# Two layers of attention: normalisation of the output split over two blocks, image loads in halves, another order of the units

## The chip, the cores and the metric

The kernel runs on one core of one Trainium2 chip. The metric is the device time of one execution in microseconds; the runs of one kernel are summed up by their median. All arithmetic is in fp32.

## The reference, cut to what matters

Each of two layers adds to x the result of an attention over the group-normalised x. There are 16 images of 256 channels and 32 x 32 positions, four heads of 64 channels.

```python
def layer(x, Wq, bq, Wk, bk, Wv, bv, rel_h, rel_w):
    xf = gn(x).reshape(b, c, n)                  # 16 groups over the last axis
    q, k, v = (W @ xf + bias, split into 4 heads of 64)
    sim  = einsum('bhdi,bhdj->bhij', q, k)
    rel  = (rel_h + rel_w).reshape(heads, d, n)
    qpos = einsum('hdi,bhdj->bhij', rel, q)
    attn = softmax(sim + qpos, axis=-1)
    out  = einsum('bhdn,bhmn->bhdm', v, attn)
    return x + out.reshape(x.shape)
x = layer(x, *layer0); x = layer(x, *layer1)
```

## The kernel before, in words

**Units and blocks.** A unit is one image in one layer, (b, l). There are 32 of them, in the order of the list `units` (line 139). A unit has four blocks: two pairs of heads (`pr`) times two halves of 512 query positions (`half`). `block(n)` (line 610) writes the instructions of block n, 128 blocks in all. Even blocks have half 0, odd blocks half 1. In an even block the text speaks of the "first" (b = 0) or "third" (b = 2) block of a unit, in an odd one of the second or fourth.

**One block.** For each of eight tiles j of 128 keys: VectorE writes the positional part of the scores into a PSUM tile (`seed`, line 344), TensorE adds k times q to it (`scores`, line 380), and ScalarE takes the exp into an SBUF tile p (line 389). `attend` (line 414) multiplies p by v into `po` in two stretches, and `take_out` (line 475) copies it into an output tile `od`. The PSUM tiles have four tags, a to d, given out by the list `ring`; a seed has to wait until the tile's former use has been read out. Beside that, each block works ahead for the next units: projections, values and positions (lines 263, 293, 321), and on ScalarE and TensorE the group norm of the units after (`norm_sums`, `norm_squares`, `norm_apply`, small matmuls `pm` at line 208). Each block holds two such pieces of projections on TensorE.

**The sums of the softmax.** VectorE adds up the p tiles of j = 0 to 6 in `acc` (`add_up`, lines 398 and 400); the add of j = 6 of an even block is issued at the start of the next block, that of an odd block at its end. POOL adds the last one by an accumulating DMA (`add_last`, line 431), then `acc` is folded over the partitions by further DMAs: `fold` (line 436), `stack_up` on SP's queue (line 450), `fold_again` (line 455), `fold_stack` (line 460, five times), `spread_sums` on SP's queue (line 468) into `den_all`. These stretch over the following three blocks.

**Normalisation.** In an even block n, for the pair of blocks n-4 and n-3 (`before`, line 616): after the scores of j = 5, `reciprocals` (line 504) takes the reciprocal on VectorE (line 511), writes it to DRAM (`rd`, line 513) and reads it back broadcast in two DMAs of 256 KB (`rden`, line 518), all three on SP's queue. Near the end of the same block `finish` (line 523) multiplies `od` by it (line 530), adds bias and residual into x (line 532) and, in layer 1, writes the result to DRAM (line 534). On VectorE's queue three seeds of the next block follow.

**Loads.** An image x is loaded by two DMAs of 512 KB (`load_x`, line 103) into one of five buffers. The load is issued in the fourth block of the unit three places ahead of the image's first unit (line 719).

**Order.** The order of the program's text is the order of each engine's queue: VectorE, ScalarE, TensorE, POOL with its DMAs, and SP with its DMAs. Each works through its queue in order, and waits at semaphores. The two stretches of a matmul group are separated by a token that POOL writes (`stretches`, line 155; `word`, line 164), so a late POOL queue can hold TensorE up. The last unit's second half has a path of its own (`block_without_pieces`, line 748), where `keep_sums` (line 492) carries sums.

Of the kernel before, what the change touches and what calls it, by code (L numbers as in the profile page):

```python
# [9 lines left out]
F32 = mybir.dt.float32  # L10
# [3 lines left out]
ALU = mybir.AluOpType  # L14
# [3 lines left out]
P = 128  # L18
HALF = 512
# [24 lines left out]
def flat(ap):  # L44
    return ap.rearrange("p w h -> p (w h)")
# [7 lines left out]
def fast_path(ctx, tc, sh, x, layers, out, W, den_all, token, good, flag):  # L53
# [26 lines left out]
    nc = tc.nc  # L80
    B, C, H, N, CC, NT, NH, D, GT = (
        sh.B, sh.C, sh.H, sh.N, sh.CC, sh.NT, sh.NH, sh.D, sh.GT
    )
# [4 lines left out]
    xpool = ctx.enter_context(tc.tile_pool(name="xpool", bufs=5))  # L88
# [4 lines left out]
    ppool = ctx.enter_context(tc.tile_pool(name="ppool", bufs=12))  # L93
# [3 lines left out]
    opool = ctx.enter_context(tc.tile_pool(name="opool", bufs=2))  # L97
# [2 lines left out]

    xt = {}

    def load_x(b):
        xt[b] = xpool.tile([P, CC, N], F32, tag="x", name=f"x_{b}")
        for cc in range(CC):
            nc.sync.dma_start(xt[b][:, cc, :], flat(x[b, cc * P : (cc + 1) * P]))

    def load_raw(name, parts):
# [27 lines left out]
            nc.scalar.copy(w.rearrange("p a c -> p (a c)"), raw_t.pop((l, part)))  # L136


    units = [(b, 0) for b in range(4)] + [(0, 1), (1, 1)]
    for b in range(4, B - 1):  # L140
        units += [(b, 0), (b - 2, 1)]
    units.insert(-1, (B - 1, 0))
    units += [(b, 1) for b in range(B - 3, B)]
    NU = len(units)
    ks, qs, abt, vts, xns = {}, {}, {}, {}, {}

# [190 lines left out]
    seeds, probs, accs, outs = {}, {}, {}, {}  # L337
# [54 lines left out]
    def add_up(blk, j):  # L392
        u, pr, half = blk
        if j == 0:
            return
        if j == 1:
            accs[blk] = apool.tile([P, 2, HALF], F32, tag="acc", name=f"acc_{u}_{pr}_{half}")
            nc.vector.tensor_tensor(accs[blk], probs[blk, 0], probs[blk, 1], ALU.add)  # L398
        else:
            nc.vector.tensor_tensor(accs[blk], accs[blk], probs[blk, j], ALU.add)  # L400

    QUART = HALF // 2
# [22 lines left out]
    index, rdens = {}, {}  # L425
# [44 lines left out]
    def take_out(blk, po):  # L470

        u, pr, half = blk
        if half == 0:
            outs[u, pr] = opool.tile([P, 3, HALF], F32, tag="od", name=f"od_{u}_{pr}")
        nc.scalar.copy(  # L475
            outs[u, pr][:, half, :].rearrange("p (a n) -> p a n", a=2), po[:, :, :QUART]
        )
# [11 lines left out]
                        start=True, stop=True, tile_position=(0, r0), skip_group_check=True,  # L489
                    )  # L490

    def keep_sums(od, po, n, count):
        rows_ = slice(0, 2 * count * R)
        nc.scalar.copy(
            od[rows_, 2, :].rearrange("p (a n) -> p a n", a=2), po[rows_, :, QUART:]
        )
        for x in range(count):
            for h in range(2):
                r0 = (2 * x + h) * R
                nc.sync.dma_start(  # L500
                    den_all[h * D : (h + 1) * D, n + x, :], od[r0 : r0 + 1, 2, :]
                )

    def reciprocals(u, pr, count=2):
# [15 lines left out]
                rd[h : h + 1].to_broadcast([D, count * HALF]),  # L520
            )

    def finish(u, pr):

        b, l = units[u]
        xs = xt[b][:, pr, :]
        od = outs.pop((u, pr))
        o = od[:, 0:2, :].rearrange("p x (k e) -> p x k e", e=8)
        rden = rdens.pop((u, pr)).rearrange("p (k x e) -> p x k e", x=2, e=8)
        nc.vector.tensor_tensor(o, o, rden, ALU.mult)  # L530
        o = od[:, 0:2, :].rearrange("p a n -> p (a n)")
        nc.vector.scalar_tensor_tensor(xs, o, W.bv[l][:, pr : pr + 1], xs, ALU.add, ALU.add)  # L532
        if l == NL - 1:
            nc.sync.dma_start(flat(out[b, pr * P : (pr + 1) * P]), xs)


    def finish_half(u, pr, half, o, rden):
# [35 lines left out]
    blocks = [(u, pr, half) for u in range(NU) for pr in range(CC) for half in range(NH)]  # L573
# [4 lines left out]
    pos = {}  # L578
# [31 lines left out]
    def block(n):  # L610
        blk = blocks[n]
        u, b = divmod(n, BPU)
        half = blk[2]

        stacked = blocks[n - 3][:2] if half == 1 and n > 2 else None
        before = blocks[n - 4][:2] if half == 0 and n > 3 else None
        after = blocks[n + 1] if n + 1 < len(blocks) else None
        previous = blocks[n - 1] if n > 0 else None
        one, two = u + 1 < NU, u + 2 < NU

        pieces = u + 1 < NU or b < 2
        if u + 1 == NU and b == 1:
            widen(u, 1)
        f0, f1, f2, f3 = ring
        folded = n - 1 < FOLDED
        if not pieces:
            return block_without_pieces(n, half)

        if stacked:
            fold_stack(*stacked, D)  # L630
        if previous:
            if half == 1:
                add_up(previous, 6)
            if folded:
                add_last(previous)
            else:
                add_up(previous, 7)
        for j in range(1, 4):
            scores(blk, j)
        (first, first_out), (second, second_out) = prepare(u, b)  # L640
        first(0)
        if b == 0 and one:
            norm_apply(u + 1, range(0, 1))
        if b == 1 and two:
            norm_sums(u + 2, range(9, 11))
        seed(blk, 4, f1)
        scores(blk, 4)
        add_up(blk, 1)
        if b == 0 and one:
            norm_apply(u + 1, range(1, 5))  # L650
        if b == 1 and two:
            norm_sums(u + 2, range(11, 12))
        if b == 2 and two:
            norm_squares(u + 2, range(0, 5))
        second(0)
        if half == 1:
            second_out()
        first.word()
        if half == 0:
            second.word()  # L660
        if stacked:
            fold_stack(*stacked, R)
        if previous and folded:
            fold(previous)
        if stacked:
            fold_stack(*stacked, R // 2)
            fold_stack(*stacked, R // 4)
        first(1)
        first_out()
        seed(blk, 5, f0)  # L670
        scores(blk, 5)
        if before:
            reciprocals(*before)
        if previous and folded:
            stack_up(previous)
        add_up(blk, 2)
        if half == 0:
            second(1)
            second_out()
        seed(blk, 6, f1)  # L680
        scores(blk, 6)
        if half == 0:
            ring[2:] = f3, f2
        seed(blk, 7, ring[2])
        scores(blk, 7)
        add_up(blk, 3)
        add_up(blk, 4)

        if after:
            seed(after, 0, f0)  # L690
        if n in check:
            next(checks)
        if b == 0 and one:
            norm_apply(u + 1, range(5, 9))
        if b == 0 and two:
            norm_sums(u + 2, range(0, 2))
        if b == 1 and two:
            norm_sums(u + 2, range(12, G))
        if b == 1 and one:
            norm_apply(u + 1, range(9, 11))  # L700
        if b == 2 and two:
            norm_squares(u + 2, range(5, 11))
        po = psum2(ring[3], f"po_{n}")
        values_of_p = attend(blk, po)
        values_of_p(0)
        if two and half == 1:
            mean, mean_out = (norm_mean if b == 1 else norm_var)(u + 2, zeroed(f1, f"pm_{n}"))
            mean(0)
        if after:
            scores(after, 0)  # L710
        values_of_p.word()
        if two and half == 1:
            mean(1)
        if stacked:
            fold_stack(*stacked, R // 8)
            spread_sums(*stacked)
        if previous and folded:
            fold_again(previous)
        if b == 3 and u + 3 < NU and units[u + 3][0] not in xt:
            load_x(units[u + 3][0])  # L720
        if two and half == 1:
            mean_out()
        add_up(blk, 5)
        if half == 1:
            add_up(blk, 6)
        if before:
            finish(*before)
        if after:
            for j in range(1, 4):
                seed(after, j, ring[j % 3])  # L730
        if b == 0 and two:
            norm_sums(u + 2, range(2, 9))
        if b == 1 and one:
            norm_apply(u + 1, range(11, G))
        if b == 2 and two:
            norm_squares(u + 2, range(11, G))
        values_of_p(1)
        take_out(blk, po)
        pos[n] = po

# [7 lines left out]
    def block_without_pieces(n, half):  # L748

        blk = blocks[n]  # L750
        u, pr, _ = blk
        f0, f1, f2, f3 = ring
        summed = blocks[n - 2][:2] if half == 0 else (u, pr)
        before = blocks[n - 4][:2] if half == 0 else blocks[n - 3][:2]
        first = index[summed + (0,)]
        add_up(blocks[n - 1], 7)
        for j in range(1, 4):
            scores(blk, j)
        sums_of_p(blocks[first:n], pos[n - 1])
        keep_sums(outs[summed], pos[n - 1], first, n - first)  # L760
        if half == 1:
            finish(*before)
        else:
# [451 lines left out]
```

## Time and profile before

| what | value |
|---|---|
| median of 3 runs | 2587.51 us (2584.55 to 2592.39) |
| profiled execution, its own time | 2584.54 us |
| its span, first to last instruction | 2582.8 us |
| granted TensorE clock, mean | 0.995 |
| busy: TensorE, weight loads | 2533.4 us (98%), 1699.2 us |
| busy: VectorE, ScalarE, POOL | 2264.9, 1959.6, 827.4 us |
| mean of the DMAs | 86 GB/s |

The profile is that of one execution. "PE" is TensorE's matmuls, "PEld" its weight loads, DVE VectorE, ACT ScalarE, POOL GpSimd, SP SyncE; "SPq" is a DMA issue on SP's queue. Groups are named by line, engine and tiles (out<-in). A matmul's end is modelled, so busy TensorE says that it was never without work, not that it ran at its peak.

### The profile page before, as it was taken

The numbers are of one execution on the slowest core, as the hardware profiler recorded it, in microseconds if no ns is written. First come the engines' busy times: TensorE is split into PE (matmuls) and PEld (weight loads), VectorE is DVE, ScalarE is ACT, GpSimd is POOL, SyncE is SP. The second block draws the span as 40 slices with busy tenths as digits, with TensorE's granted clock in tenths as the row PEclk, the third lists the DMA queues.
The fourth block names the chain that finished last, engine by engine and source line by source line (L and its number), as shares of the span: only waits on it lengthen the run. The fifth ranks groups of instructions, "written<-read, shape, count | busy, mean of one in ns | idle before, by whom it ended". The sixth has DMA issues, their size and how long they took to land. (4 is left out here: it accounts for less than half of the span.)

```text
span 2582.8 us, 86091 instructions
## 1 busy us (share of the span) xinstructions
PE 2533.4 (98%) x37474; PEld 1699.2 (66%) x37474; DVE 2264.9 (88%) x2076; ACT 1959.6 (76%) x3934; POOL 827.4 (32%) x1254
## 2 busy tenths in 40 slices
PE   8999999999999999999999999999999999999998
PEld 4666766667667655675657767676666677666654
DVE  6788888888888998978889898888898898998997
ACT  6778777787777887776877778777788777787653
POOL 1233333323333333333333332333323333323320
PEclk9999999999999999999999999999999999999999
DMA  3444444444444444444444444444444444444441
GB/s 90 81 69 79 80 86 82 91 100 78 93 86 94 90 76 99 88 87 86 80 93 87 96 83 84 99 86 91 81 81 105 93 87 82 72 83 83 87 89 49
DMA packets 119538, 221.06 MB, mean 86 GB/s; under 512 B 53736, under 2 KB 55272, under 8 KB 119152
## 3 DMA queue, kind: packets, MB, share of 16 engines
q0 software_dynamic: 53568, 129.58, 30.6%
q1 hardware_dynamic: 65584, 85.90, 12.3%
q8 instruction: 295, 4.83, 0.8%
q14 instruction: 91, 0.75, 0.1%
HBM read 51.78 MB, written 17.30 MB: 27 GB/s over the span
## 5 line engine op out<-in xcount | busy, mean ns | idle before, releaser
L344 DVE TENSOR_TENSOR ps<-abt 128x1024 f32<-128x1024 f32 x1018 | 1222.3, 1229 | 232.2 <-ACT p L389 66.3
L389 ACT ACTIVATE p<-ps,shift 128x1024 f32<-128x1024 f32 x1024 | 1094.2, 1114 | 348.4 <-PE ps L380 257.4
L380 PE MATMUL ps<-q,k 64*64 64x512 f32 x8192 | 1027.1, 594 | 17.9 <-DVE ps L344 17.2
L414 PE MATMUL po<-p,v 64*64 64x256 f32 x16384 | 945.8, 376 | 0.1
L414 PEld LDWEIGHTS po<-p,v 64*64 64x64 f32 x16384 | 807.1, 133 | 155.3 <-issue 44.6
L400 DVE TENSOR_TENSOR acc<-acc,p 128x1024 f32<-128x1024 f32 x644 | 781.9, 1214 | 7.3
L380 PEld LDWEIGHTS ps<-q,k 64*64 64x64 f32 x8192 | 396.1, 133 | 344.8 <-issue 173.6
L460 POOL DMA_DIRECT2D stack<-stack x310 | 254.0, 819 | 498.9 <-DMA stack<-stack 262.7
L164 POOL MEMSET token<- 1x1 f32 x380 | 43.4, 114 | 861.5 <-PE po L414 488.0
L293 PE MATMUL pv<-Wv,xn 64*64 64x256 f32 x4096 | 251.4, 376 | 0.3 <-DVE var L868 0.3
L263 PE MATMUL pq<-xn,Wq 64*64 64x512 f32 x2048 | 251.3, 592 | 0.3 <-DVE xn L900 0.3
L263 PE MATMUL pk<-xn,Wk 64*64 64x512 f32 x2048 | 248.9, 590 | 0.0
L455 POOL DMA_DIRECT2D stack<-acc x248 | 225.1, 1111 | 71.9 <-DMA stack<-acc 50.5
L293 PEld LDWEIGHTS pv<-Wv,xn 64*64 64x64 f32 x4096 | 201.2, 133 | 56.1 <-issue 41.5
L243 ACT ACTIVATE xn<-x,nshift,rstd 128x128 f32<-128x128 f32 x496 | 210.9, 500 | 9.7 <-POOL nshift L234 9.7
L188 ACT ACTIVATE junk<-x,neg 128x128 f32<-128x128 f32 x498 | 195.1, 401 | 0.0
L263 PEld LDWEIGHTS pq<-xn,Wq 64*64 64x64 f32 x2048 | 107.7, 134 | 113.0 <-issue 108.5
L436 POOL DMA_DIRECT2D acc<-acc x124 | 102.3, 825 | 241.1 <-DMA acc<-p 219.2
L475 ACT COPY od<-po 128x512 f32<-128x512 f32 x127 | 74.4, 586 | 128.4 <-PE po L414 119.9
L263 PEld LDWEIGHTS pk<-xn,Wk 64*64 64x64 f32 x2048 | 98.4, 134 | 102.9 <-issue 101.8
L431 POOL DMA_DIRECT2D acc<-p x124 | 143.4, 1156 | 50.4 <-ACT p L389 40.1
L398 DVE TENSOR_TENSOR acc<-p,p 128x1024 f32<-128x1024 f32 x128 | 156.2, 1221 | 0.1
(75 smaller groups left out, 1231.3 us busy)
## 6 DMA issues: line engine op xcount, KB each, us to landing
acc<-p POOLq DMA_DIRECT2D x124, 512.0 KB, 5.3
rden<-rd SPq DMA_DIRECT2D x126, 256.0 KB, 4.7
acc<-acc POOLq DMA_DIRECT2D x124, 256.0 KB, 3.9
x<-in_x_dram SPq DMA_DIRECT2D x32, 512.0 KB, 4.6
stack<-acc SPq DMA_DIRECT2D x248, 64.0 KB, 2.1
stack<-acc POOLq DMA_DIRECT2D x248, 64.0 KB, 2.9
out_dram<-x SPq DMA_DIRECT2D x31, 512.0 KB, 3.5
stack<-stack POOLq DMA_DIRECT2D x62, 128.0 KB, 2.7
```

The source lines that it names most:

```text
L188: nc.scalar.activation(junk, grouped(xt[units[u][0]], g), func, accum_out=into[:, g : g + 1], **bias)
L243: nc.scalar.activation(grouped(xns[u], g), grouped(xt[units[u][0]], g), AF.Identity, bias=shift[:, g : g + 1], scale=rstd[:, g : g + 1],)
L263: yield nc.tensor.matmul(pk[c, nh, :], w[l][rs, cc, c0 : c0 + D], xns[u][rs, cc, nh * HALF : (nh + 1) * HALF], start=(t == 0 and cc == 0), ...
L293: yield nc.tensor.matmul(pv[c, a, i, :], xns[u][rs, cc, j0 : j0 + D], W.wv[l][rs, cc, :], start=(t == 0 and cc == 0 and i == 0), stop=(t = ...
L344: nc.vector.tensor_tensor(ps.rearrange("p h (w y) -> p h w y", y=H), ab[:, :, :H].unsqueeze(2).to_broadcast([P, 2, XH, H]), ab[:, :, H + h ...
L380: nc.tensor.matmul(ps[c, h, :], a[hs, j0 : j0 + D], b[hs, columns], start=bool(tag) and i == 0, stop=i == len(terms) - 1, skip_group_check ...
L389: nc.scalar.activation(p, ps, AF.Exp, bias=W.shift)
L398: nc.vector.tensor_tensor(accs[blk], probs[blk, 0], probs[blk, 1], ALU.add)
L400: nc.vector.tensor_tensor(accs[blk], accs[blk], probs[blk, j], ALU.add)
L414: yield nc.tensor.matmul(po[c, a, :QUART], vts[u][rs, j, c0 : c0 + D], p[rs, h, a * QUART : (a + 1) * QUART], start=(t == 0 and j == 0), s ...
L455: nc.gpsimd.dma_start(at, acc[R:D, h, :], accum_op=ALU.add)
L460: nc.gpsimd.dma_start(stack[:rows_], stack[rows_ : 2 * rows_], accum_op=ALU.add)
```

## The change

The order of the units is rewritten: some layer-1 units come earlier, others later. Images are loaded one half per odd block instead of both in the fourth block. `finish` is split: `normalise` near the start of the odd block n, `add_residual` near its end, for the pair of blocks n-5 and n-4. `reciprocals` moves within the even block from after the scores of j = 5 to after the adds of j = 3 and 4. The add of j = 6 is issued at the start of the next block for odd blocks also. `od` tiles have two parts of 512 instead of three and three buffers instead of two; the sums kept at the end lie in a p tile.

```diff
@@ -100,9 +100,10 @@
 
     xt = {}
 
-    def load_x(b):
-        xt[b] = xpool.tile([P, CC, N], F32, tag="x", name=f"x_{b}")
-        for cc in range(CC):
+    def load_x(b, parts=range(CC)):
+        if 0 in parts:
+            xt[b] = xpool.tile([P, CC, N], F32, tag="x", name=f"x_{b}")
+        for cc in parts:
             nc.sync.dma_start(xt[b][:, cc, :], flat(x[b, cc * P : (cc + 1) * P]))
 
     def load_raw(name, parts):
@@ -136,11 +137,12 @@
             nc.scalar.copy(w.rearrange("p a c -> p (a c)"), raw_t.pop((l, part)))
 
 
-    units = [(b, 0) for b in range(4)] + [(0, 1), (1, 1)]
-    for b in range(4, B - 1):
+
+    units = [(b, 0) for b in range(4)] + [(0, 1), (1, 1), (4, 0), (2, 1), (3, 1), (5, 0)]
+    for b in range(6, B - 4):
         units += [(b, 0), (b - 2, 1)]
-    units.insert(-1, (B - 1, 0))
-    units += [(b, 1) for b in range(B - 3, B)]
+    units += [(B - 6, 1), (B - 4, 0), (B - 3, 0), (B - 5, 1), (B - 2, 0), (B - 1, 0)]
+    units += [(b, 1) for b in range(B - 4, B)]
     NU = len(units)
     ks, qs, abt, vts, xns = {}, {}, {}, {}, {}
 
@@ -471,7 +473,7 @@
 
         u, pr, half = blk
         if half == 0:
-            outs[u, pr] = opool.tile([P, 3, HALF], F32, tag="od", name=f"od_{u}_{pr}")
+            outs[u, pr] = opool.tile([P, 2, HALF], F32, tag="od", name=f"od_{u}_{pr}", bufs=3)
         nc.scalar.copy(
             outs[u, pr][:, half, :].rearrange("p (a n) -> p a n", a=2), po[:, :, :QUART]
         )
@@ -489,16 +491,15 @@
                         start=True, stop=True, tile_position=(0, r0), skip_group_check=True,
                     )
 
-    def keep_sums(od, po, n, count):
+    def keep_sums(po, n, count):
         rows_ = slice(0, 2 * count * R)
-        nc.scalar.copy(
-            od[rows_, 2, :].rearrange("p (a n) -> p a n", a=2), po[rows_, :, QUART:]
-        )
+        d = ppool.tile([P, 2, HALF], F32, tag="p", name=f"d_{n}")[:, 0, :]
+        nc.scalar.copy(d[rows_].rearrange("p (a n) -> p a n", a=2), po[rows_, :, QUART:])
         for x in range(count):
             for h in range(2):
                 r0 = (2 * x + h) * R
                 nc.sync.dma_start(
-                    den_all[h * D : (h + 1) * D, n + x, :], od[r0 : r0 + 1, 2, :]
+                    den_all[h * D : (h + 1) * D, n + x, :], d[r0 : r0 + 1, :]
                 )
 
     def reciprocals(u, pr, count=2):
@@ -520,18 +521,23 @@
                 rd[h : h + 1].to_broadcast([D, count * HALF]),
             )
 
-    def finish(u, pr):
+    def normalise(u, pr):
+        o = outs[u, pr].rearrange("p x (k e) -> p x k e", e=8)
+        rden = rdens.pop((u, pr)).rearrange("p (k x e) -> p x k e", x=2, e=8)
+        nc.vector.tensor_tensor(o, o, rden, ALU.mult)
+
+    def add_residual(u, pr):
 
         b, l = units[u]
         xs = xt[b][:, pr, :]
-        od = outs.pop((u, pr))
-        o = od[:, 0:2, :].rearrange("p x (k e) -> p x k e", e=8)
-        rden = rdens.pop((u, pr)).rearrange("p (k x e) -> p x k e", x=2, e=8)
-        nc.vector.tensor_tensor(o, o, rden, ALU.mult)
-        o = od[:, 0:2, :].rearrange("p a n -> p (a n)")
+        o = outs.pop((u, pr)).rearrange("p a n -> p (a n)")
         nc.vector.scalar_tensor_tensor(xs, o, W.bv[l][:, pr : pr + 1], xs, ALU.add, ALU.add)
         if l == NL - 1:
             nc.sync.dma_start(flat(out[b, pr * P : (pr + 1) * P]), xs)
+
+    def finish(u, pr):
+        normalise(u, pr)
+        add_residual(u, pr)
 
 
     def finish_half(u, pr, half, o, rden):
@@ -610,10 +616,11 @@
     def block(n):
         blk = blocks[n]
         u, b = divmod(n, BPU)
-        half = blk[2]
+        pr_, half = blk[1:]
 
         stacked = blocks[n - 3][:2] if half == 1 and n > 2 else None
-        before = blocks[n - 4][:2] if half == 0 and n > 3 else None
+        summed = blocks[n - 4][:2] if half == 0 and n > 3 else None
+        before = blocks[n - 5][:2] if half == 1 and n > 4 else None
         after = blocks[n + 1] if n + 1 < len(blocks) else None
         previous = blocks[n - 1] if n > 0 else None
         one, two = u + 1 < NU, u + 2 < NU
@@ -629,14 +636,15 @@
         if stacked:
             fold_stack(*stacked, D)
         if previous:
-            if half == 1:
-                add_up(previous, 6)
+            add_up(previous, 6)
             if folded:
                 add_last(previous)
             else:
                 add_up(previous, 7)
         for j in range(1, 4):
             scores(blk, j)
+        if before:
+            normalise(*before)
         (first, first_out), (second, second_out) = prepare(u, b)
         first(0)
         if b == 0 and one:
@@ -669,8 +677,6 @@
         first_out()
         seed(blk, 5, f0)
         scores(blk, 5)
-        if before:
-            reciprocals(*before)
         if previous and folded:
             stack_up(previous)
         add_up(blk, 2)
@@ -685,6 +691,8 @@
         scores(blk, 7)
         add_up(blk, 3)
         add_up(blk, 4)
+        if summed:
+            reciprocals(*summed)
 
         if after:
             seed(after, 0, f0)
@@ -716,15 +724,13 @@
             spread_sums(*stacked)
         if previous and folded:
             fold_again(previous)
-        if b == 3 and u + 3 < NU and units[u + 3][0] not in xt:
-            load_x(units[u + 3][0])
+        if half == 1 and u + 3 < NU and units[u + 3][1] == 0 and u > 0 or n == 3:
+            load_x(units[u + 3][0], range(pr_, pr_ + 1) if u > 0 else range(CC))
         if two and half == 1:
             mean_out()
         add_up(blk, 5)
-        if half == 1:
-            add_up(blk, 6)
         if before:
-            finish(*before)
+            add_residual(*before)
         if after:
             for j in range(1, 4):
                 seed(after, j, ring[j % 3])
@@ -753,11 +759,13 @@
         summed = blocks[n - 2][:2] if half == 0 else (u, pr)
         before = blocks[n - 4][:2] if half == 0 else blocks[n - 3][:2]
         first = index[summed + (0,)]
+        if half == 0:
+            add_up(blocks[n - 1], 6)
         add_up(blocks[n - 1], 7)
         for j in range(1, 4):
             scores(blk, j)
         sums_of_p(blocks[first:n], pos[n - 1])
-        keep_sums(outs[summed], pos[n - 1], first, n - first)
+        keep_sums(pos[n - 1], first, n - first)
         if half == 1:
             finish(*before)
         else:
```

## The prediction

> **What bounds the kernel now.** I read the page first, then the waits, the timelines of the engines and the windows of single stretches.
>
> ```profile
> PE 2533.4 (98%) x37474; PEld 1699.2 (66%) x37474; DVE 2264.9 (88%) x2076; ACT 1959.6 (76%) x3934; POOL 827.4 (32%) x1254
> ...
> rden<-rd SPq DMA_DIRECT2D x126, 256.0 KB, 4.7
> acc<-acc POOLq DMA_DIRECT2D x124, 256.0 KB, 3.9
> x<-in_x_dram SPq DMA_DIRECT2D x32, 512.0 KB, 4.6
> ```
>
> TensorE is busy nearly throughout, so the change can win only what TensorE loses in stalls. To size that I took from ScalarE's timeline the start of the second exp (tile p of j=1) of each of the 128 blocks; below T is that moment of the even block of a pair (half 0), and T+20.66 that of its odd block. Undisturbed, the four blocks of a unit take 20.66, 18.26, 20.64 and 18.28 us, together 77.84 us. The windows of such blocks show no gap at all:
>
> ```profile
> 2177.26:2197.93 20.67, 20.67 (x292) 13.96 (x288) 17.86 (x17) 17.39 (x39) 7.65 (x10) 1.00 0.44 82
> 2197.93:2216.20 18.27, 18.27 (x300) 11.89 (x296) 17.25 (x17) 15.83 (x34) 8.13 (x13) 1.00 0.45 77
> ```
>
> The first column after the window is its length, the second TensorE's busy time: they are equal, so no reordering makes such a block shorter. What the first 31 units take beyond that is 44.2 us: 19.4 in first, 20.5 in second, 4.3 in fourth blocks of a unit, nothing in third ones. The last unit adds 91.8 us with gaps of its own. The waits name two causes:
>
> ```profile
> PEld ps L380 <- DVE ps L344: 150.7, 335, 4.2
> PEld pm L208 <- POOL token L164: 42.2, 60, 3.7
> DVE od L530 <- DMA rden<-rd: 32.2, 18, 5.0
> DVE r L511 <- DMA den_all<-stack: 19.2, 22, 2.1
> ```
>
> (waiter, releaser: total us, times, longest.) **Stall A**: VectorE waits at `finish` for the broadcast reciprocals `rden`; the seeds of the next block are queued behind it, and TensorE waits for the seeds. The worst case is the first block of unit 14:
>
> ```profile
> 1155.60 1.22 DVE L400 TENSOR_TENSOR acc<-acc,p 128x1024 f32<-128x1024 f32 x1
> 1161.86 1.23 DVE L530 TENSOR_TENSOR od<-od,rden 128x1024 f32<-128x1024 f32 x1 [5.04 <-DMA rden<-rd]
> 1163.12 1.28 DVE L532 SCALAR_TENSOR_TENSOR x<-od,bv,x 128x1024 f32<-128x1024 f32 x1
> 1164.33 3.50 DVE L344 TENSOR_TENSOR ps<-abt 128x1024 f32<-128x1024 f32 x3
> ```
>
> ```profile
> 1163.00:1165.50 2.50, 0.00 (x0) 0.00 (x0) 2.46 (x4) 0.59 (x1) 1.69 (x2) 0.76 0.30 57
> 1165.50:1171.00 5.50, 5.39 (x28) 1.71 (x32) 5.50 (x6) 2.23 (x2) 1.74 (x2) 0.50 0.49 130
> ```
>
> TensorE stands still and then works at half its clock (0.50). All large A stalls are in the first block of a unit, which follows a load of two 512 KB halves of x. Here rden was asked for early and came late because its predecessor `rd` (8 KB) landed only with the 512 KB accumulate `acc<-p` of the same block:
>
> ```profile
> 1155.49 0.84 POOL L436 DMA_DIRECT2D acc<-acc  x1 [7.17 <-DMA acc<-p]
> ```
>
> SP's timeline has the two rden issues at 1155.38, just when that accumulate ended. **Stall B**: in an odd block, the second stretch of the small matmul `pm` waits for a token that POOL writes only after a string of stack folds; a fold chain that starts late delays it. From first and fourth blocks' excess and the gap that opens each, I assign A 27 us (19.4 plus about 8 that spill into the following block) and B 17 us.
>
> [...] a wait of 4.2 us was followed by 0.50, a wait of 2.1 us was not. [...]
>
> **The change, part by part.**
>
> 1. *Residual in two parts, one block later; add of j=6 of odd blocks one block later.* VectorE's work per pair is the same; it moves. Occupancies from the timeline: seed or add 1.14, normalise 1.26, residual 1.20, reciprocal 0.17. Even block before: 8 seeds, 5 adds, reciprocal, finish: 17.4 us of 20.66; odd: 8 seeds, 7 adds: 17.1 of 18.26. After: even 8+6, reciprocal: 16.1; odd 8+6, finish: 18.4 of 18.26. The odd block overruns by 0.1 us, so it must start early, and it can. The clean pair reads
>
> ```profile
> 2190.71 1.22 DVE L400 TENSOR_TENSOR acc<-acc,p 128x1024 f32<-128x1024 f32 x1
> 2192.26 1.23 DVE L530 TENSOR_TENSOR od<-od,rden 128x1024 f32<-128x1024 f32 x1 [0.33 <-DMA rden<-rd]
> 2193.52 1.29 DVE L532 SCALAR_TENSOR_TENSOR x<-od,bv,x 128x1024 f32<-128x1024 f32 x1
> 2194.72 3.50 DVE L344 TENSOR_TENSOR ps<-abt 128x1024 f32<-128x1024 f32 x3
> 2198.12 1.22 DVE L400 TENSOR_TENSOR acc<-acc,p 128x1024 f32<-128x1024 f32 x1
> 2199.26 1.23 DVE L344 TENSOR_TENSOR ps<-abt 128x1024 f32<-128x1024 f32 x1
> ```
>
> Without finish, the first two of the three seeds follow at 2191.9; the third waits for the exp of score 0 (ends 2194.73), so it runs 2194.8 to 2195.9, the add of j=6 to 2197.1, normalise to 2198.3. Seed 4 cannot start before the exp of score 1 ends (2199.04); it starts now at 2199.26. So normalise fits, with about 0.9 us over: it may start as late as T+20.75 without moving a seed. Later costs TensorE one for one, since seed 7 is ready now only some 0.1 us before its score. The residual takes the place of the moved add (1.20 for 1.14) ahead of a 0.96 us idle. In the even block the moved add sits before seed 4, which then ends about 0.44 us before its score. Cost: 0. Bounds: 0 to 0.3 us in each of 62 pairs, if these margins fail.
>
> 2. *Reciprocal later.* It now comes after the add of j=4, at T+12.3 instead of T+4.6; the three DMAs follow on SP behind stack_up, which waits for POOL's fold. Today the fold is issued at T+6.5 (third block) or T+7 to 8.5 (first block) and takes 3.4 us alone, 4.4 to 5.3 with rden in flight; stack_up issues at T+10 to 14. With rden gone from there I take 3.4 us. First block: fold T+8.6, stack_up T+12.1 and 12.6, rd T+13.2, landing 1.6 later at T+14.8, two rden landing 4.9 after the first issue: T+19.7. Third block: the moved add delays acc<-p from T-2 to T+1.6, it lands at about T+6.6 to 7.8, so the fold is hardly later; rden lands at T+18.5 to 19. Both are ahead of T+20.75, by 1.0 and 2 us. Not shown by the trace is rden in that slot: 4.4 us at best (in three blocks, where the fold was missing or came late, both had landed 4.4 to 4.6 after the first issue), 6.4 at worst as beside a fold: T+19.2 to T+21.2. The reciprocal's own wait of 19.2 us ends; it was covered mostly. A goes: -27. I keep +4: x of image 3 is still loaded whole before block 4, where the chain gives about 1.3 us late, and some loads start late.
>
> 3. *Loads in halves.* 512 KB instead of 1 MB start before an even block. With 1 MB ahead, acc<-p took 6.3 to 9.7 us instead of 4.7 in eleven of twelve cases; I estimate 5.0 to 6.5 with half. The out DMAs move too: behind the later residual and SP's spread and load, they leave at the start of the next even block instead of at T+17. In the alternating part, units that load and units that write alternate, so there is one 512 KB transfer per even block. Both are inside the fold time taken above.
>
> 4. *B.* The accumulate of the even block no longer waits until T+22.3 for the add of j=6; that add ends 2.2 us earlier, so its fold clears earlier in the chain, and the out DMA that slowed fold_again (landing at T+22 instead of T+19.7) is gone. Against it, rden now runs beside fold_again: about 1 us, absorbed by POOL's own wait for TensorE at T+24. I take -17 and keep +5.
>
> 5. *Order of units, three od buffers, sums kept in a p tile.* ScalarE's 8.5 us of waits for od end, unseen by TensorE. Every load finds a buffer freed at least a block before. The tail: normalise joins `widen`, but finish left the block before; one more add ahead of the sums of the next: within 0.5 us, taken as 0.
>
> Sum against the profiled execution, 2584.5 (span 2582.8 and 1.7 around it): 2584.5 - 27 + 4 - 17 + 5 = 2549.5. It lies 3.0 us under the median of the runs shown (2587.5), so a median may be 0 to 3 us higher: I say 2551.
>
> **Rivals.** *Slower: rden comes too late for normalise.* The chain is now serial: fold, stack_up, rd, rden in 7.5 us after the reciprocal, where it had 10 us before. If the new slot is as crowded as the old one in first blocks (fold 5.3, rd 3.5, rden 5.9), rden lands at T+24; halfway to that, at T+22.75, 31 first blocks lose 2.0 us each: 2549.5 + 62 = 2612. The gain is gone from a mean lateness of 0.57 us over 62 pairs (35/62). For it: SP's strict order. Against it: the fold and the accumulate, which held rd and rden up, have landed by then. *Half gain:* lateness of some 0.5 us in first blocks (+15) and B only halved (+4): 2569. *No effect:* new collisions of loads and writes at the start of even blocks make stalls as large as the old ones: about 2585.
>
> **How the numbers follow.** Forecast 0.64 (2540 to 2561), half gain 0.18 (to 2579), no effect 0.04, slower 0.14. A measurement of this kernel can tell about 0.3%, 7.8 us, from no change: faster 0.82, same 0.05, slower 0.13. The range 2538 to 2579 holds the first two.
>
> **What would show it.** Right: no wait of `od` on rden over 1 us after block 4, rden landing before T+20.75, reciprocal's wait gone, clock never 0.50 between 200 and 2400 us, PE waits for POOL's token in `pm` below half of 42 us. Wrong: waits of normalise on rden in most odd blocks, or acc<-p landing beyond T+10 in many first blocks.

## The result, and the profile after

| | before | changed |
|---|---|---|
| median of 5 runs | 2585.83 us (2583.91 to 2592.39) | 2566.39 us (2564.16 to 2574.49) |
| profiled execution, its time | 2584.54 us | 2564.16 us |
| its span | 2582.8 us | 2562.4 us |
| mean granted clock | 0.995 | 0.998 |

The ratio is 0.9928, with a 95% interval of 0.9907 to 0.995: faster by 0.7%. The forecast was 2551, in a range of 2538 to 2579: it lies inside, but the gain is 19 us where 35 were forecast.

Measured by the same block starts as before the change, the first 31 units exceed 31 x 77.84 us, here called the floor, by 23.8 us instead of 44.2. First blocks, which had 19.4 us of excess, have 0.7; fourth blocks have 8.2 instead of 4.3, second ones 14.9 instead of 20.5. So the stalls at the end of even blocks are gone, but the odd blocks together still lose 23.1 us where they lost 24.8. The waits of the changed kernel (waiter, releaser: total us, times, longest) say by what:

```profile
PEld ps L382 <- DVE ps L346: 145.1, 303, 2.9
DVE od L527 <- DMA rden<-rd: 54.5, 37, 3.7
PEld pm L210 <- POOL token L166: 27.3, 60, 2.9
```

The wait of VectorE for the broadcast reciprocals, 32.2 us in 18 places before, is now 54.5 us in 37 places; the wait of the reciprocal for the sums (19.2 us) is gone. The token waits of the small matmuls fell from 42.2 to 27.3 us; these are waits of the weight loads, which start ahead of their matmuls (by 0.28 us at the median of these 60 waits in the changed kernel). TensorE's own waits there, before and after, show that almost all of them now cost nothing:

```profile
PE pm L208 <- POOL token L164: 9.3, 11, 2.8
PE pm L210 <- POOL token L166: 2.0, 1, 2.0
```

The half clock is gone too: in the kernel before, TensorE ran at 0.50 in three stretches of the first 31 units, 13.7 us in all (after stalls that began at 687, 1162 and 1799 us); in the changed kernel the clock is 1.00 throughout from 32 to 2470 us. A group of four matmuls of the scores starts every 0.85 us in such a stretch and every 0.43 us outside (kernel before, from 1166 and from 2180 us), so about half of the 13.7 us, some 7 of the 44.2, can be put down to it (an estimate). The DMA rows of the page show the fold and the broadcast each faster (3.9 and 4.7 us before). They no longer overlap: rden was in flight beside 61 of the 124 folds before, which took 5.0 us at the median against 3.4 for the other 63, and is beside none now:

```profile
rden<-rd SPq DMA_DIRECT2D x126, 256.0 KB, 4.0
acc<-acc POOLq DMA_DIRECT2D x124, 256.0 KB, 3.5
```

Where rden is punctual, VectorE's order is the one that was worked out. This is its timeline at the end of the first block of unit 14 (T = 1136.42), the place of the worst stall before:

```profile
1151.15 2.36 DVE L346 TENSOR_TENSOR ps<-abt 128x1024 f32<-128x1024 f32 x2
1153.92 1.23 DVE L346 TENSOR_TENSOR ps<-abt 128x1024 f32<-128x1024 f32 x1 [0.41 <-ACT p L391]
1155.06 1.22 DVE L402 TENSOR_TENSOR acc<-acc,p 128x1024 f32<-128x1024 f32 x1
1156.20 1.22 DVE L527 TENSOR_TENSOR od<-od,rden 128x1024 f32<-128x1024 f32 x1
1158.23 1.23 DVE L346 TENSOR_TENSOR ps<-abt 128x1024 f32<-128x1024 f32 x1 [0.81 <-ACT p L391]
```

Two seeds, the third after ScalarE's exp, the moved add, normalise at T+19.78, and then 0.81 us of room before seed 4. In the first block of unit 7 (T = 585.89) the room did not suffice. VectorE, then SP's and POOL's queues:

```profile
604.53 1.22 DVE L402 TENSOR_TENSOR acc<-acc,p 128x1024 f32<-128x1024 f32 x1
607.86 1.23 DVE L527 TENSOR_TENSOR od<-od,rden 128x1024 f32<-128x1024 f32 x1 [2.11 <-DMA rden<-rd]
609.00 1.23 DVE L346 TENSOR_TENSOR ps<-abt 128x1024 f32<-128x1024 f32 x1
```

```profile
587.03 0.58 SPq L107 DMA_DIRECT2D x<-in_x_dram  x1
587.71 0.38 SPq L536 DMA_DIRECT2D out_dram<-x  x1
599.37 1.15 SPq L452 DMA_DIRECT2D stack<-acc  x2
600.61 0.54 SPq L514 DMA_DIRECT2D rd<-r  x1
602.27 2.21 SPq L519 DMA_DIRECT2D rden<-rd  x2
```

```profile
587.80 0.93 POOL L433 DMA_DIRECT2D acc<-p  x1 [0.22 <-issue]
...
595.89 0.84 POOL L438 DMA_DIRECT2D acc<-acc  x1 [3.82 <-DMA acc<-p]
```

A load and a write of 512 KB each leave just ahead of the accumulate. That lands 7.8 us after its issue, the fold follows at T+10.0, stack_up at T+13.5 (599.37), rd at T+14.7 although the reciprocal was ready at T+12.5 (598.4), rden at T+16.4. Normalise starts at T+21.97, and TensorE loses 1.1 us at seed 4. Normalise may start as late as T+20.88 without a loss; what it starts later than that is called its lateness below. Over the 60 pairs it sums to 21.2 us.

### The profile page after: what moved, and what is told of

Its sections match the earlier page's. It is cut to its first block, busy times and chain, and to the rows that moved or that the text cites. A ratio compares the mean times of both kernels' runs of the same rounds, so it can differ in the third digit from the quotient of the medians.

```text
span 2562.4 us, 86058 instructions
## 1 busy us (share of the span) xinstructions
PE 2528.3 (99%) x37474; PEld 1625.7 (63%) x37474; DVE 2253.2 (88%) x2076; ACT 1955.8 (76%) x3934; POOL 837.8 (33%) x1254
## 4 chain that ended last, share of the span: by engine, by line
PE 77%; DMA 9%; DVE 9%; issue 3%; POOL 1%; SPq 1%; ACT 1%; DVEq 0%; POOLq 0%; ACTq 0%
PE po L416 28%; PE ps L382 27%; PE pv L295 7%; PE pq L265 7%; PE pk L265 6%; DVE ps L346 5%; DMA rden<-rd 3%; DMA acc<-p 2%; DVE acc L402 2%; PE pa L323 2%; DMA rd<-r 2%; DMA acc<-acc 1%; DVE acc L400 1%; POOL rstd L234 0%; SPq L452 0%
## 5 line engine op out<-in xcount | busy, mean ns | idle before, releaser
L416 PEld LDWEIGHTS po<-p,v 64*64 64x64 f32 x16384 | 775.8, 133 | 186.6 <-issue 44.4
L382 PEld LDWEIGHTS ps<-q,k 64*64 64x64 f32 x8192 | 372.7, 133 | 357.1 <-issue 177.7
L295 PEld LDWEIGHTS pv<-Wv,xn 64*64 64x64 f32 x4096 | 189.9, 133 | 67.4 <-issue 44.2
L265 PEld LDWEIGHTS pq<-xn,Wq 64*64 64x64 f32 x2048 | 100.4, 134 | 120.3 <-issue 114.1
L433 POOL DMA_DIRECT2D acc<-p x124 | 131.4, 1059 | 122.9 <-DVE acc L402 115.5
```

Of the source, the lines that this page charges most:

```text
L265: yield nc.tensor.matmul(pk[c, nh, :], w[l][rs, cc, c0 : c0 + D], xns[u][rs, cc, nh * HALF : (nh + 1) * HALF], start=(t == 0 and cc == 0), ...
L295: yield nc.tensor.matmul(pv[c, a, i, :], xns[u][rs, cc, j0 : j0 + D], W.wv[l][rs, cc, :], start=(t == 0 and cc == 0 and i == 0), stop=(t = ...
L382: nc.tensor.matmul(ps[c, h, :], a[hs, j0 : j0 + D], b[hs, columns], start=bool(tag) and i == 0, stop=i == len(terms) - 1, skip_group_check ...
L416: yield nc.tensor.matmul(po[c, a, :QUART], vts[u][rs, j, c0 : c0 + D], p[rs, h, a * QUART : (a + 1) * QUART], start=(t == 0 and j == 0), s ...
```

## The experiments

Two theories were put to the test. **Theory 1**: what is left of stall A comes from the place of the reciprocal. Its DMAs stand in SP's queue behind stack_up, so behind the fold and the accumulate, and these are late where they meet loads and writes. **The rival**: the later place is what makes the change work, since it keeps the fold clear of rden; the rest is loads and writes alone. Medians are of the runs of each kernel; ratios are against the kernel before on the same chip.

**The reciprocal alone put back.**

```diff
         scores(blk, 5)
+        if summed:
+            reciprocals(*summed)
         if previous and folded:
             stack_up(previous)
...
         add_up(blk, 4)
-        if summed:
-            reciprocals(*summed)
```

> The changed kernel with the reciprocal and its three DMAs put back to where they were (after the scores of j=5, ahead of stack_up on SP's queue); the rest of the change stays. Theory 1 (the rest of stall A, about 20 us in the changed kernel, comes from queueing rd and rden behind acc<-p, fold and stack_up): rden lands by T+20 in every pair, VectorE's waits of normalise fall from 54 us to under 5, and the time is 2546 to 2553. Rival (the later reciprocal is what keeps the fold free of rden; put back, the fold takes 4.4 to 5.3 us instead of 3.4 and the token waits of odd blocks return): no wait for rden, but 2562 or more.

Measured: 2553.16 us, ratio 0.9878 (0.9863 to 0.9893). rden landed at T+14 in the median, and VectorE waited for it once, 2.5 us in the last unit, where the changed kernel has 54.5 us in 37 places. The fold in even blocks took 4.7 us again (median), as the rival says. But the fold's delay cost little: of the 15.4 us of excess over the floor 12.9 lie in five odd blocks with token waits (5.3 of them in block 29, which has a stretch of 3.4 us at half clock) and 1.6 in the even block 40. Theory 1 holds, 0.2 us above its range: the later reciprocal costs about 13 us.

**Loads whole.**

```diff
-        if half == 1 and u + 3 < NU and units[u + 3][1] == 0 and u > 0 or n == 3:
-            load_x(units[u + 3][0], range(pr_, pr_ + 1) if u > 0 else range(CC))
+        if b == 3 and u + 3 < NU and units[u + 3][1] == 0:
+            load_x(units[u + 3][0])
```

> The changed kernel with both halves of an image loaded together in the fourth block. Theory 1: the accumulate acc<-p of about 12 first blocks lands at T+9 to T+13 as before the change, the serial chain behind it brings rden 2 to 5 us late there, and the third blocks gain about 8 us back; in sum 2575 to 2592, with half-clock stretches. Rival (halving the loads matters little, since two 512 KB transfers take as long apart as together): 2564 to 2570.

Measured: 2584.94 us, ratio 0.9994 (0.9982 to 1.0006). The late reciprocal with whole loads is no faster than the kernel before. The rival, with 2564 to 2570, is out. Its premise about two transfers was the author's assumption; in the traces two halves issued together had landed 5.1 to 9.8 us after the first issue (kernel before, from 113 us on), and a half issued by itself took 3.7 to 7.2 us (changed kernel, from 311 us on). Stall A has merely moved by a block: second blocks now lose 43.8 us. The waits of VectorE show the cause, and the windows show the half clock after one of the long stalls (third number from the right is the clock):

```profile
DVE od L527 <- DMA rden<-rd: 63.7, 31, 6.6
```

```profile
609.00:612.00 3.00, 0.00 (x0) 0.00 (x0) 2.41 (x3) 0.00 (x0) 1.80 (x3) 0.75 0.40 66
612.00:617.00 5.00, 4.98 (x80) 2.75 (x84) 4.68 (x5) 2.43 (x4) 2.41 (x3) 0.50 0.69 121
```

**The kernel before with the order and the halves alone.** These are the change's own lines for the order and the halves, without the reciprocal, the split and the moved add:

```diff
-    def load_x(b):
+    def load_x(b, parts=range(CC)):
...
-    units = [(b, 0) for b in range(4)] + [(0, 1), (1, 1)]
-    for b in range(4, B - 1):
+    units = [(b, 0) for b in range(4)] + [(0, 1), (1, 1), (4, 0), (2, 1), (3, 1), (5, 0)]
+    for b in range(6, B - 4):
...
-        if b == 3 and u + 3 < NU and units[u + 3][0] not in xt:
-            load_x(units[u + 3][0])
+        if half == 1 and u + 3 < NU and units[u + 3][1] == 0 and u > 0 or n == 3:
+            load_x(units[u + 3][0], range(pr_, pr_ + 1) if u > 0 else range(CC))
```

> The kernel before with the new order of units and the loads in halves alone; reciprocal and finish as before. Theory 1: rd no longer waits for more than T+10 or so behind acc<-p, so rden is at most some 2 us late; A falls from 27 us to about 8, B stays near 17: 2563 to 2570. Rival (the gain of the change is from moving finish, not from loads): 2582 to 2588.

Measured: 2566.03 us, ratio 0.9932 (0.9918 to 0.9945). This alone is as fast as the whole change. VectorE's waits for rden fell from 32.2 to 10.4 us; stall B stayed, with 42.9 us of token waits in `pm` (the profiled execution, 2561.54 us, was the fastest of the five). No stretch at half clock was left.

**The split and the order, loads whole, reciprocal early.** The two edits above, of the reciprocal and of the loads, together:

```diff
+        if summed:
+            reciprocals(*summed)
         if previous and folded:
             stack_up(previous)
...
-        if summed:
-            reciprocals(*summed)
...
+        if b == 3 and u + 3 < NU and units[u + 3][1] == 0:
+            load_x(units[u + 3][0])
```

> The changed kernel with the reciprocal early and the loads whole: of the change, the residual in two parts a block later and the new order. Theory 1: rden landed by T+19.7 at worst before the change, and normalise may wait until T+20.9, so stall A is gone even with whole loads: 2546 to 2558. Rival (halved loads are needed as well): waits for rden of 1 to 3 us in first blocks after a load, or folds so late that the token holds TensorE: 2565 to 2580.

Measured: 2559.6 us, ratio 0.9905 (0.989 to 0.992), 1.6 us above the range of theory 1. No pair had a late rden. The whole loads still cost 6.4 us against the same kernel with halves (2553.16). The trace puts it to stall B, with 48.3 us of token waits against 35.1; but the execution that was profiled took 2567.35 us, 7.8 above the median, so its 48.3 is that of a bad case.

**One order on SP's queue swapped.**

```diff
-        if previous and folded:
+        if previous and folded and half == 1:
             stack_up(previous)
...
             reciprocals(*summed)
+        if previous and folded and half == 0:
+            stack_up(previous)
```

> The changed kernel with one order on SP's queue swapped in even blocks: the late reciprocal's rd and rden come first, stack_up after them. VectorE's order is that of the changed kernel. Theory 1 (rden is late because rd queues behind stack_up, hence behind the fold and acc<-p, not because the reciprocal itself comes late on VectorE): rd issues at T+12.6 in every pair, rden lands by T+19.5, waits of normalise fall from 54 us to under 8; stack_up moves to T+15.3, which costs some of stall B back: 2548 to 2560. Rival (the reciprocal at T+12.3 is itself too late, or rden is slowed by fold_again): waits of normalise stay above 30 us and the time at 2562 or more.

Measured: 2705.12 us, ratio 1.0465 (1.0441 to 1.0489). The first half of the expectation came true, the second was far off.

```profile
PEld pm L210 <- POOL token L166: 139.6, 60, 6.0
...
DVE od L527 <- DMA rden<-rd: 9.9, 13, 2.6
```

With rd issued at T+12.6, rden was late in 3 pairs, and the summed lateness of normalise fell from 21.2 to 2.6 us: so the reciprocal's place on VectorE is not at fault, the queue ahead of rd is. But stack_up's two DMAs now issue at T+15.6 and T+16.3 (medians), and the first takes 3.7 us to land instead of 2.0, behind rden on the same queue; fold_again moves from T+16.1 to T+20.0, and the chain of folds behind it delays the token in nearly every odd block: 172 us in 62 odd blocks, 2.8 us each. About 34 us of this can be put down to the half clock, an estimate from 68 us of stretches at 0.50 in this run and from the 0.85 us in place of 0.43 above. What remains is 2.2 us per block for 3.9 us of delay, so that chain has less than 2 us to spare. I had priced the swap at a few us in all.

**Image 3 in halves too**, with the early reciprocal.

```diff
-        if half == 1 and u + 3 < NU and units[u + 3][1] == 0 and u > 0 or n == 3:
-            load_x(units[u + 3][0], range(pr_, pr_ + 1) if u > 0 else range(CC))
+        if half == 1 and u + 3 < NU and units[u + 3][1] == 0:
+            load_x(units[u + 3][0], range(pr_, pr_ + 1))
```

> The early-reciprocal kernel with image 3 loaded in halves too, like all others. Theory: the token wait of block 5 (1.4 us) comes from that 1 MB load ahead of the accumulate and goes: 1 to 2 us less than the early-reciprocal kernel, 2551 to 2552.5. Rival (an opening effect of the first units): no change, 2553 to 2554.

Measured: 2553.78 us, ratio 0.9881 (0.9859 to 0.9904), against 0.9878 without: no difference. The stall of block 5 went, as expected, but others were longer in this execution (block 96: 2.1 us instead of 0.4). The effect is too small to be told here.

**The add of j = 6 back in its own odd block**, with the late reciprocal.

```diff
-            add_up(previous, 6)
+            if half == 1:
+                add_up(previous, 6)
...
         add_up(blk, 5)
+        if half == 1:
+            add_up(blk, 6)
...
-        if half == 0:
-            add_up(blocks[n - 1], 6)
```

> The changed kernel with the add of j=6 of odd blocks back at the end of its own block; all else as changed. Theory 1: acc<-p of third blocks is issued at T-2 again instead of T+2.1, its fold at T+6.5 instead of T+8.1, so rd issues at T+12.6 and the 8 us lost in fourth blocks go, while VectorE's longer odd block costs 0 to 0.3 us per pair: 2556 to 2566. Rival (the odd block is then bound by VectorE: 19.6 us of work in 18.3, about 1.2 us lost per pair): 2600 to 2640.

Measured: 2557.53 us, ratio 0.9898 (0.9874 to 0.9921). Fourth blocks lost 2.5 us instead of 8.2, and the lateness of third blocks' pairs fell from 8.2 to 0.6 us. The longer odd block cost VectorE nothing visible; the next block starts with one add less. The rival is out. Moving that add was a loss of 8 to 9 us beside the late reciprocal; the size is uncertain, since this interval and the changed kernel's (0.9907 to 0.995) overlap, though the times of the runs do not (at most 2561.88 here, at least 2564.16 there).

**Loads at mid-block**, once with the early and once with the late reciprocal; image 3 comes in halves in both.

```diff
             stack_up(previous)
+        if half == 1 and u + 3 < NU and units[u + 3][1] == 0:
+            load_x(units[u + 3][0], range(pr_, pr_ + 1))
         add_up(blk, 2)
...
-        if half == 1 and u + 3 < NU and units[u + 3][1] == 0 and u > 0 or n == 3:
-            load_x(units[u + 3][0], range(pr_, pr_ + 1) if u > 0 else range(CC))
```

> The early-reciprocal kernel with image 3 in halves and each half loaded right behind the odd block's stack_up (about T_odd+10) instead of at its end, so that it has landed before the next block's accumulate. Theory: what is left of stall B (5.3, 3.5, 2.1 us in blocks 29, 97, 21) comes from loads and writes meeting the accumulate at the start of the even block; most of it goes: 2540 to 2547. Rival (the load now meets the stack folds of the odd block and delays the token in many of them): 2553 to 2565.

Measured: 2546.46 us, ratio 0.9853 (0.9831 to 0.9875). The kernel of the experiment on image 3 differs from it by the place of the loads alone: 2553.78 us there, and 13.4 us of excess over the floor against 6.3 here. The 4.8 us of block 29 are gone. So about half of the excess that was left came from loads ahead of the accumulate.

> The changed kernel, reciprocal late as in it, with one edit: each half of an image (image 3 too) is loaded right behind the odd block's stack_up instead of at its end. Theory 1a (the spread of rden's lateness comes from acc<-p landing late where it meets a load at the start of the even block): late pairs that follow a load become punctual; the summed lateness falls from 21 us to about 8, the rest being blocks with an out DMA or without either: 2550 to 2558. Rival (the serial queue is late by itself, the loads don't matter once halved): lateness stays at 17 or more, 2562 to 2568.

Measured: 2559.98 us, ratio 0.9897 (0.988 to 0.9913), halfway between the two expectations. The summed lateness fell from 21.2 to 15.8 us only, nearer to the rival's 17. The 17 pairs that had had a load alone lost 3.6 us instead of 6.9, of which 2.1 is image 3 in halves; the eight with a load and a write 7.2 instead of 9.9; the other 35 lost 5.1 instead of 4.4. Pairs with a write ahead of them make up 10.5 of the 15.8 us. So loads are one part of the spread; with the serial queue, lateness has other sources too, above all in pairs that follow a write.

**The two best put together, and the write first.** To the kernel with early reciprocal and loads at mid-block, the add of j = 6 in its own block, by the edit above; and, apart from that, the spread DMAs moved behind the residual and its out DMA:

```diff
             fold_stack(*stacked, R // 8)
-            spread_sums(*stacked)
...
         if before:
             add_residual(*before)
+        if stacked:
+            spread_sums(*stacked)
```

> The kernel with early reciprocal and loads at mid-block, plus the add of j=6 of odd blocks back in its own block. Theory: with the early reciprocal nothing waits for the third block's fold by less than some us, so an earlier acc<-p there gains nothing on rden; the token waits may lose 0 to 2 us, VectorE's longer odd block costs 0 to 1: 2544 to 2548, no difference that can be told. Rival: the odd block's seeds come late, 2550 or more.

Measured: 2544.26 us, ratio 0.9842 (0.9827 to 0.9856), the fastest of all and as expected, though not to be told from 0.9853. Its 3.9 us of excess over the floor leave little to win in these units:

```profile
PE 2513.9 (99%) x37474; PEld 1662.0 (65%) x37474; DVE 2261.6 (89%) x2076; ACT 1956.4 (77%) x3934; POOL 824.7 (32%) x1254
```

> The kernel with early reciprocal and loads at mid-block, plus SP's out DMA ahead of the four spread DMAs, so that it has landed before the next block's accumulate. Theory: at most the 6 us of stalls that are left can go, and only those of blocks 77 and 97, which follow a write: 2543 to 2546. Rival (the spread, held behind the residual, makes the reciprocal wait for den_all and the write meets the last folds): 2548 to 2556.

Measured: 2546.84 us, ratio 0.9852 (0.9835 to 0.9868), between the two expectations and the same as without the edit (0.9853): no gain, and blocks 77 and 97 kept 1.0 and 1.4 us. The guess that the write causes those two stalls is not supported.

## Why the prediction was right in its direction and short in its size

Step by step, in the prediction's own numbering:

- **Step 1, the moved work on VectorE: right.** Normalise starts at T+19.75 when rden is there, and in late pairs TensorE's loss is normalise's start less T+20.88, pair by pair (block 28: 1.08 us late, 1.08 us of excess; block 68: 1.53 and 1.52); 20.75 was forecast as the limit. Restoring the add cost VectorE nothing that shows.
- **Step 2, the chain to rden: right in the middle, wrong in the spread.** This is the term that failed, the +4 kept of stall A. The medians came out as worked: in first blocks fold T+8.5 (8.6 forecast), second stack_up T+12.5 (12.6), rd T+13.2 (13.2), rden T+20.5 (19.7); in third blocks rden T+19.8 (18.5 to 19). But the margin of 1 us was smaller than the scatter: 20 of 60 pairs were late by over 0.2 us, and the lateness sums to 21.2 us where 4 were allowed. Of it, 9.9 us belong to 8 pairs that have a load and a write ahead of them, with rden at T+22.0 on average; 6.9 us to 17 pairs with a load alone (2.1 us of it to image 3, whose load is whole); and 4.4 us to 35 pairs with a write alone or with neither. The prediction also read 6.4 us as the longest pair of rden; the trace before has up to 7.7. That did no harm, since in the new slot a pair took 5.6 at most.
- **Step 3, one 512 KB transfer per even block: wrong for those 8 pairs.** I had checked the alternating part of the order and not its two irregular stretches (units 6 to 9 and 20 to 23), where loads and writes share blocks. There the accumulate took 7.1 us in the median (4.9 to 7.8); with a load alone 5.9 (half of an image 4.6 to 7.4, mostly inside the estimate), with a write alone 5.0, with neither 4.6. That the moved add "hardly" delays the fold was wrong too: it is nearly all of the 8.2 us of lateness in third blocks, of which its restoration left 0.6.
- **Step 4, stall B: right.** Of 17 us some 3 are left (23.8 of excess less 21.2 of lateness), nearly all in block 21; 5 were allowed. The sign I had named for it was a bad one: the token waits of `pm` fell to 27.3 us and not below half of 42, but the fastest kernel of all, with 3.9 us of excess, still has 27.4. In that kernel the 60 waits of the weight loads, 0.46 us each on average, cost TensorE next to nothing (its own waits there are 2.6 us).
- **Step 5: right**, the tail from block 124 on takes 91.7 us, as before (91.8).

With the measured terms the sum is 2584.5 - 27 + 21 - 17 + 3 = 2564.5; the profiled execution took 2564.2. The mechanism of the slower rival was the one at work, at a mean lateness of 21.2/62 = 0.34 us and not the 0.57 from which it would have decided. The result lies where the half-gain rival put it, but for half of its reason only: first blocks were late by 0.43 us on average, as it says, but third blocks were late too, and B was not halved but nearly gone.

Of the signs that were named, two came out for right (the reciprocal's wait gone, the clock never 0.50). Against it, rden landed after T+20.75 in 24 of 60 pairs, and normalise waited for it in 36, mostly by over 1 us, which had been named as a sign of being wrong; the accumulate landed beyond T+10 in two first blocks only. One working of the prediction does not come out: halfway from its own T+19.7 to T+24 is T+21.85, not T+22.75; 31 first blocks would then lose 1.1 us each, 34 us, which makes that rival a draw and not a loss of 27 us.

What each part is worth follows from the ratios, added in this order: order and halves -0.7%; on top of them the split (with its moved add) another -0.5%; and the later reciprocal gives +0.5% back. That last part is the one whose worth the forecast had not separated. The worths depend on each other: the halves bring 0.7% beside the late reciprocal (0.9994 with whole loads to 0.9928) and 0.3% beside the early one (0.9905 to 0.9878). Not settled: where the last 4 to 6 us of excess in the best kernels come from, most of it in blocks 21, 77 and 97; and how much of the -0.7% is due to the order alone, which the loads in halves need for free buffers and which was not run by itself. Nor were the third od buffer and the sums in a p tile run alone.

## What to carry to other kernels

When a step is moved later on one engine, look at where its DMAs then stand in the issuing queue. Here the later reciprocal took its three DMAs behind stack_up, and stack_up's wait for a fold set their time, not the step: in unit 7 the reciprocal was ready at T+12.5 and rd was issued at T+14.7, and in the kernel with the swapped order, with stack_up behind it, rd was issued at T+12.6. When a chain is timed against a deadline, compare the margin with the scatter of the chain, block by block, and not with its median: median margins of 0.3 us in first blocks and 1.1 us in third ones still lost 21 us in 60 pairs. And two orders on one queue that look exchangeable can have very different slack behind them, as the swap of stack_up and rden showed (2705.12 us against 2566.39).

## What the runs showed of the hardware that I had not expected

- A small DMA landed late behind earlier ones. In the changed kernel, rd (8 KB) took 1.4 us at best and 1.6 in the median, and in 44 of 60 pairs it landed within 0.3 us after the last of stack_up's 64 KB. It is not the whole story: the three slowest, 3.3 to 3.5 us, landed about 2 us after stack_up was through, and why is open. In the kernel before, the two slowest rd, 8.4 and 8.5 us (issued at 1147.01 and 1783.81 us), landed 0.2 us after the 512 KB accumulate on POOL's queue that was in flight beside them. With rden ahead on the same queue, in the kernel with the swapped order, the first DMA of stack_up took 3.7 us instead of 2.0.
- A fold of 256 KB took 3.45 us with no rden in flight (changed kernel, median of 124), 5.0 us beside two rden in the kernel before and 4.7 us with the early reciprocal; the two rden took 5.0 us, from the first issue to the last landing, beside fold_again (changed kernel) and 6.1 beside the fold (kernel before). Separating them gained 1.1 to 1.6 us on each, and still lost time in all.
- How long TensorE stood still did not decide by itself whether half clock followed. In the kernel with the swapped order on SP's queue, a stall of 1.9 us was followed by 0.50 for 3.4 us, and one of 3.2 us was not (the third number from the right is the clock):

```profile
2115.52:2117.44 1.92, 0.00 (x1) 0.00 (x0) 0.00 (x0) 1.11 (x1) 0.93 (x3) 1.00 0.16 36
2118.30:2121.70 3.40, 3.40 (x40) 3.40 (x34) 3.40 (x4) 0.00 (x0) 2.60 (x4) 0.50 0.13 16
942.30:945.50 3.20, 0.00 (x1) 0.00 (x1) 0.01 (x1) 1.11 (x1) 0.93 (x3) 1.00 0.17 42
945.50:950.00 4.50, 4.50 (x80) 4.13 (x84) 3.86 (x4) 0.86 (x2) 2.96 (x4) 1.00 0.17 20
```

The kernel before has such a pair too: a stall of 2.5 us at 687 us was followed by half clock, one of 2.8 us at 463 us was not.

```profile
687.34:689.86 2.52, 0.00 (x1) 0.00 (x1) 2.48 (x4) 0.59 (x1) 1.69 (x2) 1.00 0.30 57
689.86:693.20 3.34, 3.34 (x16) 0.99 (x20) 3.34 (x4) 1.11 (x1) 0.56 (x1) 0.50 0.50 166
463.21:466.00 2.79, 0.00 (x1) 0.00 (x0) 0.12 (x1) 1.11 (x1) 0.93 (x3) 1.00 0.35 66
466.00:471.00 5.00, 5.00 (x84) 4.44 (x88) 3.50 (x3) 3.01 (x8) 3.43 (x4) 1.00 0.27 41
```

So the prediction's two waits, 4.2 us with half clock after it and 2.1 us without, do not give a length from which a stall is followed by half clock. What decides beside the length is not shown here.
